# A state-space convolution by three products of 128-blocks in place of four, beside a quantized FFN

## The chip, the cores and the metric

The kernel runs on one core of one Trainium2 chip. The metric is the device time of one execution in microseconds (us), the median of several runs. The core has five engines with their own instruction queues: TensorE (PE, with its weight loads shown as PEld), VectorE (DVE), ScalarE (ACT), GpSimd (POOL) and SyncE (SP), which here only issues transfers. Engines wait for each other through semaphores.

## The reference, cut to what matters

The input `x` is 2048 rows (tokens) of 1024. The output is `x` plus two branches of its layer norm:

```
xn = layernorm(x)
x  = x + s4(xn) + ffn(xn)

# s4: K (1024 numbers) from the state matrices; D is one number
y = irfft(rfft(u, 2L) * rfft(K, 2L), 2L)[..., :L]      # causal convolution along the 1024 columns
s4 = y + D * u

# ffn: hidden 1024, inter 2752, int4 weights with a scale and zero per group of 64
h = silu(u @ Wg.T) * (u @ Wu.T)
ffn = h @ Wd.T
```

So each row is convolved with the same 1024 taps `K`: a product with an upper triangular Toeplitz matrix of 1024 x 1024. Cut into 128-blocks it has one block per diagonal, T0 to T7, and output block j is the sum over i <= j of x_i T(j-i).

## The kernel before, in words

The kernel is written in Python; a planner (the Tile framework) allocates buffers, adds semaphores and orders each engine's queue by the order of the program, a model of time, and hand-made order edges (`tc.issue_after`). Every number in a product is kept as a sum of two f16 numbers (high and low), and each product is three matmuls (`PASS`: high·high, high·low, low·high).

**Weights and FFN, to about 846 us.** The layer norm, the int4 unpacking and the gate and up products (`gate_up`) run here; `h` goes to HBM (`HF`, `HPL`), the down weights to `WD2`. In between, in small steps, `s4_kernel` computes `K` on 8 partitions; it ends with two tiny f32 matmuls into `s4k` and the stores of the split taps to HBM (`KP`, 128 zeros ahead of 1024 taps).

**The convolution, from 846.6 to 966.3 us.** This is the part that changes. It runs in two passes `cp` of 1024 rows. In a pass, `c` is a half of 512 rows, `q` one of its four tiles of 128 rows, and `hh` the half of the 1024 columns that is written, so there are 32 tiles of 128 x 512.

- `band` is loaded from `KP` with overlapping reads, four transfers on SP: its partition p is the tap vector shifted by p, so that any 128-block T_d is a slice of it.
- `diff` are two tables, differences of slices of `band`, built by DVE and ACT (`add_split`: three DVE instructions, an ACT cast and a DVE subtraction).
- `xs` are sums of blocks of `x` (blocks k and k + 2 of the first column half), two per `c`, built by the same `add_split`.
- `conv` opens a tile of 512 columns in a PSUM bank: the diagonal part as a staircase of four blocks (512, 384, 256 and 128 columns), and for hh = 1 the cross part with `diff`: four products of 256 columns. The cross part of 512 x 512 is thus done with three products of 256-blocks for four: two with difference tables, one shared.
- `last_tiles` adds five matmuls of 512 columns with `hpl` and `wp` (the last part of the FFN's down product), loads `x` into `o` (SP), and DVE evicts the bank onto it (`p<-cv`). For hh = 1 a second bank `pc` gets the shared product (`cc<-band,xs`, six matmuls of 256), which DVE adds to both halves of `o` (`p<-cc`). SP stores `o`.

In pass 0 `last_tiles` lags four tiles behind `conv` (list `behind`), in pass 1 none. The order of (c, hh) is (0,0), (0,1), (1,1), (1,0) in pass 0 and (0,1), (0,0), (1,1), (1,0) in pass 1. Each pass first loads `hpl` (768 KB, ACT's queue) and `x7` (1 MB, SP's queue), the transposed input of c = 1, hh = 0; the other three transposed inputs are in SBUF.

**The products, from 966.3 us.** 49 products of the FFN's down projection by a recursive scheme (`items`). `operands` loads `a` and, for the third product (m = 6), makes `s` and two differences on DVE; `gsplit` makes `g` (an ACT cast, a DVE subtraction). `prepare`, called once after each four tiles of pass 1, does this ahead for the first four.

**What is scarce.** PSUM has 8 banks, all in pool `psb`. Pool `f` has 6 buffers of 10 KB per partition, for `x7`, `xs`, `a` and `s`. Pool `hb` (tag `h`) has 10 of 2 KB, for `diff`, the temporaries `t` and `o`. Pool `g` has 5, `be` 3 (`band` and `wp`).

Lines: the profile shows nearly all instructions of the convolution under L77 and L82, the two lines of the helper `Engine` that issue them, so they are told apart by names: `cv`, `cc`, `xs`, `t`, `p`. POOL's instructions carry their own lines.

Of the kernel before, what the change touches and what calls it, by code (L numbers as in the profile page):

```python
# [24 lines left out]
F16 = mybir.dt.float16  # L25
# [4 lines left out]
ALU = mybir.AluOpType  # L30
# [57 lines left out]
def build(nc, tc, x, xp, raw_d, sz_d, par_d, vct_d, tab_d, csrow_d, out):  # L88
# [3 lines left out]
    with es:  # L92
# [13 lines left out]
        KP = dr.tile([2, 1280], F16, name="KP")  # L106

# [3 lines left out]
        def bank(name, tag="ps"):  # L111
            return psp.tile([P, 512], F32, tag=tag, name=name, **({} if tag == "ps" else {"bufs": 2}))
# [175 lines left out]
        with ea:  # L288
# [518 lines left out]
            def s4_kernel():  # L807
# [45 lines left out]
                tab, z, tab2 = tab[:, 0:512], tab[:, 512:896], tab2[:, 0:272]  # L853
                SP.dma_start(tab, tab_d[0])
                SP.dma_start(tab2[0:8], tab_d[1, 0:8, 0:272])
# [6 lines left out]
                yield "read"  # L862
                tc_, ts_ = tab2[0:8, 0:128], tab2[0:8, 128:256]
# [9 lines left out]
                pk = bank("s4k")[0:8, 0:128]  # L873
                with tc.issue_after(ends[0].ins):
                    PE.matmul(pk, tab2[0:8, 256:264], z[0:8, 0:128], start=True, stop=False)
                PE.matmul(pk, tab2[0:8, 264:272], z[0:8, 128:256], start=False, stop=True)
                yield "read"
                k = z[:, 256:384]
                V.tensor_copy(k[0:8], pk)
                V.scalar_tensor_tensor(k[0:1, 0:1], sm[0:1, 24:25], KS, k[0:1, 0:1], M, AD)  # L880
                kh = cst.tile([8, 2, P], F16, tag="s4kh", name="s4kh")
                split(kh, k[0:8])
# [4 lines left out]
                SP.dma_start(KP[:, 128:1152].rearrange("a (b c) -> b a c", b=8), kh)  # L887
# [296 lines left out]

        band = bep.tile([P, 2, 1024], F16, tag="be", name="band")
        for b in range(2):
            for n in range(2):
                p0 = 64 * b + 32 * n
                base = KP[:, 128 - 64 * b - 62 - n :]
                src = bass.AP(base.tensor, base.offset, [[2, 32], [base.ap[0][0], 2], [1, 1024]])  # L1190
                SP.dma_start(band[p0 : p0 + 32], src)

        def add_split(dst, srcs, op):

            (h0, l0), (h1, l1) = srcs
            n = dst.shape[2]
            t = htile("t")[:, 0:n]
            V.tensor_tensor(t, h0, h1, op)
            V.tensor_tensor(t, t, l0, ALU.add)
            V.tensor_tensor(t, t, l1, op)  # L1200
            A.copy(dst[:, 0], t)
            V.tensor_tensor(dst[:, 1], t, dst[:, 0], ALU.subtract)


        diff = []
        for a0, b0 in ((128, 384), (640, 384)):
            a, b = ([band[:, i, c : c + 384] for i in range(2)] for c in (a0, b0))
            diff.append(htile(f"diff{a0}").bitcast(F16).rearrange("p (a b) -> p a b", a=2)[:, :, 0:384])
            add_split(diff[-1], (a, b), ALU.subtract)
# [4 lines left out]

        def conv(cp, c, hh, q, xc):

            ts = slice(q * P, (q + 1) * P)
            ps = bank(f"cv{cp}{c}{hh}{q}")
            first = [True]

            def mm(dst, w, m):
                PE.matmul(dst, w, m, start=first[0], stop=False, skip_group_check=True)
                first[0] = False

            xt = xc[2 * c + hh]
            for k in range(4):
                for xi, bi in PASS:
                    mm(ps[:, P * k : 512], xt[:, xi, k, ts], band[:, bi, 0 : 512 - P * k])
            if hh:

                xt = xc[2 * c]
                for k in range(2):
                    for xi, bi in PASS:
                        mm(ps[:, 0:256], xt[:, xi, k + 2, ts], diff[0][:, bi, P - P * k : P - P * k + 256])
                for k in range(2):
                    for xi, bi in PASS:
                        mm(ps[:, 256:512], xt[:, xi, k, ts], diff[1][:, bi, P - P * k : P - P * k + 256])
            return ps

        def last_tiles(ps, cp, c, hh, q, hpl, xs):  # L1240

            ts = slice(q * P, (q + 1) * P)
            cols = slice(512 * hh, 512 * hh + 512)
            mm = lambda w, m, stop=False: PE.matmul(ps, w, m, start=False, stop=stop, skip_group_check=True)
            for hi, wi in PASS:
                mm(hpl[:, c, hi, ts], wp[0][:, wi, cols])
            mm(hpl[:, c, 2, ts], wp[1][:, 0, cols])
            mm(hpl[:, c, 2, ts], wp[1][:, 1, cols], True)
            t0 = 1024 * cp + 512 * c + P * q
            o = htile(f"p{cp}{c}{hh}{q}")  # L1250
            SP.dma_start(o, x[t0 : t0 + P, cols])
            V.scalar_tensor_tensor(o, ps, osc, o, ALU.mult, ALU.add)
            if hh:
                pc = bank(f"cc{cp}{c}{q}")
                for k in range(2):
                    for n, (xi, bi) in enumerate(PASS):
                        PE.matmul(pc[:, 0:256], xs[:, c, xi, k, ts], band[:, bi, 512 - P * k : 768 - P * k],
                                  start=(k == 0 and n == 0), stop=(k == 1 and n == 2))
                ov = o.rearrange("p (a b) -> p a b", a=2)
                V.scalar_tensor_tensor(  # L1260
                    ov, pc[:, 0:256].unsqueeze(1).to_broadcast([P, 2, 256]), osc, ov, ALU.mult, ALU.add)
            SP.dma_start(out[t0 : t0 + P, cols], o)
# [11 lines left out]

        for cp in range(2):
            home, tag = (gp, "g") if cp else (cvp, "cv")
            hpl = home.tile([P, 2, 3, 512], F16, tag=tag, name=f"hpl{cp}")
            A.dma_start(hpl, HPL[cp])
            x7 = fp.tile([P, 2, 4, 512], F16, tag="f", name=f"x7_{cp}")
            SP.dma_start(x7, XSP[cp])  # L1280
            xc = [xf[cp, 3], xf[cp, 1], x7, xf[cp, 0]]
            xs = fp.tile([P, 2, 2, 2, 512], F16, tag="f", name=f"xs{cp}")
            for c in range(2):
                for k in range(2):
                    a, b = ([xc[2 * c][:, i, m, :] for i in range(2)] for m in (k, k + 2))
                    add_split(xs[:, c, :, k, :], (a, b), ALU.add)

            behind = []
            for c, hh in ((0, 0), (0, 1), (1, 1), (1, 0)) if cp == 0 else ((0, 1), (0, 0), (1, 1), (1, 0)):
                for q in range(4):  # L1290
                    behind.append((conv(cp, c, hh, q, xc), cp, c, hh, q))
                    if len(behind) > 4 - 4 * cp:
                        last_tiles(*behind.pop(0), hpl, xs)
                if cp:
                    prepare()
            while behind:
                last_tiles(*behind.pop(0), hpl, xs)
# [207 lines left out]
```

## Time and profile before

| | |
|---|---|
| median of the runs shown | 1292.74 us (1290.92 to 1292.90, 3 runs) |
| profiled execution, own time | 1293.54 us |
| its span, first to last instruction | 1291.5 us |
| granted TensorE clock | 0.994 over the span, 1.00 in the convolution |
| PE busy | 1258.9 us, 97% |
| DVE, ACT, POOL busy | 1007.7, 672.1, 177.4 us |
| convolution | 846.60 to 966.34 us, 832 matmuls |
| DVE `p<-cv` x32, `p<-cc` x16 | 0.69 us each |
| DVE `t<-x` f32 from f16, 128x512 | 0.69 us |
| DVE `xs<-t,xs` f16, 128x512 | 0.69 us |
| ACT cast `xs<-t` 128x512 | 0.62 us |
| POOL add of 128x16 (line 323) | 0.22 us (median), up to 1.12 |
| POOL select of 128x128 (line 125) | 0.28 us |
| load `p<-in_x`, 256 KB | 3.7 us from issue to landing |
| load `x<-XSP`, 1 MB | 6.8 and 9.4 us from issue to landing |

How to read the profile: a row names the engine, the line, the operation, `out<-in` by the program's names, the shapes and the count; times are in us from the span's start; a bracket gives how long the engine had been idle and which instruction or transfer ended that. PE rows overlap, since matmuls are pipelined and their ends are modelled: what a matmul costs is the distance from its start to the next one's.

### The profile page before, as it was taken

Reading aid. Unit: us, or ns where it says so; the run is one execution under the profiler, and the core shown is the slowest. Engines: PE = TensorE matmul, PEld = TensorE weight load, DVE = VectorE, ACT = ScalarE, POOL = GpSimd, SP = SyncE. Lnnn points to the kernel's source line nnn. Section 1 sums busy time; section 2 is a strip of 40 time slices with the busy share of each in tenths; the row PEclk is TensorE's granted clock in tenths of the full one; section 3 lists DMA queues with packets and bytes.
Section 4 is the critical chain, followed back from the end, with each engine's and each line's share of the span. In section 5 each row is a group of like instructions: output and inputs, shape, how many; then the busy total and the mean of one; then the engine's idle time right before and its main releaser. Section 6 shows DMA issues by size and latency. Waiting matters only on the chain. (4 is left out here: it accounts for less than half of the span.)

```text
span 1291.5 us, 20871 instructions
## 1 busy us (share of the span) xinstructions
PE 1258.9 (97%) x7880; PEld 753.2 (58%) x7880; DVE 1007.7 (78%) x1344; ACT 672.1 (52%) x1208; POOL 177.4 (14%) x267
## 2 busy tenths in 40 slices
PE   5999999999999999999998999999999999999998
PEld 5744344444444444444443444456668888888887
DVE  6789974888978788878788887663758898779792
ACT  4868476666657556656666675620105433443330
POOL 2230010200010000100010001000000131356440
PEclk8999999999999999999999999999999999999999
DMA  6692938789795959889998998775938778999981
GB/s 222 147 227 59 203 101 157 213 218 239 162 252 144 253 146 241 224 209 235 244 239 216 260 243 201 226 264 183 350 122 344 239 230 226 256 283 259 288 176 50
DMA packets 358401, 276.04 MB, mean 214 GB/s; under 512 B 211668, under 2 KB 304668, under 8 KB 354204
## 3 DMA queue, kind: packets, MB, share of 16 engines
q1 hardware_dynamic: 335676, 261.59, 74.1%
q0 software_dynamic: 21760, 10.49, 6.9%
q10 hardware_dynamic: 864, 2.62, 0.5%
q8 instruction: 62, 1.02, 0.3%
q14 instruction: 39, 0.32, 0.1%
HBM read 132.36 MB, written 94.84 MB: 176 GB/s over the span
## 5 line engine op out<-in xcount | busy, mean ns | idle before, releaser
L82 PEld LDWEIGHTS <-wf 128*128 128x128 f16 x2807 | 274.0, 98 | 341.0 <-issue 7.0
L77 PEld LDWEIGHTS <-g 128*128 128x128 f16 x2940 | 287.7, 98 | 33.5
L82 ACT ACTIVATE w<-w,sz 128x64 f32<-128x64 int32 x560 | 196.0, 428 | 68.4 <-DVE w L82 51.3
L77 ACT CAST g<-a 128x2560 f16<-128x2560 f32 x42 | 97.5, 2324 | 176.6 <-PE A L77 50.4
L82 PE MATMUL D<-x,wf 128*128 128x512 f16 x816 | 188.0, 380 | 0.9 <-ACT D L82 0.9
L77 PE MATMUL A<-b,g 128*128 128x256 f16 x1680 | 185.9, 273 | 0.0
L82 PE MATMUL A<-x,wf 128*128 128x512 f16 x791 | 177.7, 380 | 5.1 <-DMA wf<-nat 4.7
L82 PE MATMUL C<-x,wf 128*128 128x512 f16 x804 | 179.1, 379 | 0.0
L82 DVE TENSOR_TENSOR w<-w 128x256 f32<-128x256 f32 (+1 forms) x244 | 132.6, 544 | 39.5 <-ACT w L82 32.3
L77 PEld LDWEIGHTS <-wf 128*128 128x128 f16 x1152 | 100.1, 100 | 98.4 <-DMA wf<-nat 4.3
L77 DVE TENSOR_TENSOR g<-a,g 128x2560 f16<-128x2560 f32 x42 | 118.5, 2823 | 29.6 <-ACT g L77 29.6
L1357 POOL DMA_DIRECT2D out<-o x64 | 78.8, 2127 | 320.7 <-DVE o L77 309.8
L82 ACT CAST nd<-w 128x896 f16<-128x896 f32 x70 | 65.2, 932 | 82.8 <-DVE w L82 65.6
L322 POOL TENSOR_SCALAR sz<-sz 128x16 f32<-128x16 f32 x42 | 16.5, 392 | 632.8 <-DMA sz<-in_sz 586.5
L77 PE MATMUL D<-b,g 128*128 128x256 f16 x840 | 94.0, 273 | 0.0
L82 PE MATMUL B<-x,wf 128*128 128x512 f16 x396 | 90.9, 379 | 2.1 <-ACT B L82 2.1
L82 DVE TENSOR_TENSOR nd<-w,nd 128x896 f16<-128x896 f32 x70 | 76.1, 1086 | 9.2 <-ACT nd L82 9.2
L82 ACT CAST nat<-w 128x896 f16<-128x896 f32 x62 | 55.2, 936 | 34.1 <-ACT B L82 17.0
L77 PEld LDWEIGHTS <-x 128*128 128x128 f16 x576 | 53.4, 98 | 25.0 <-issue 1.1
L82 DVE TENSOR_TENSOR nat<-w,nat 128x896 f16<-128x896 f32 x62 | 64.8, 1085 | 1.5 <-ACT nat L82 1.5
L77 PE MATMUL cv<-band,x 128*128 128x512 f16 (+3 forms) x384 | 57.1, 299 | 1.0 <-DVE hb L82 1.0
L77 DVE SCALAR_TENSOR_TENSOR p<-cv,p 128x512 f32<-128x512 f32 x32 | 22.0, 689 | 43.3 <-PE cv L77 33.6
(169 smaller groups left out, 1408.6 us busy)
## 6 DMA issues: line engine op xcount, KB each, us to landing
a<-HF SPq DMA_DIRECT2D x28, 1280.0 KB, 8.0
WD<-nd SPq DMA_DIRECT2D x70, 448.0 KB, 4.1
b<-WD SPq DMA_DIRECT2D x49, 640.0 KB, 6.0
w<-SZT SPq DMA_DIRECT2D x80, 256.0 KB, 5.4
raw<-in_raw SPq DMA_DIRECT2D x65, 256.0 KB, 4.0
HF<-ha SPq DMA_DIRECT2D x54, 256.0 KB, 3.4
HF<-s SPq DMA_DIRECT2D x40, 256.0 KB, 2.8
HF<-hb SPq DMA_DIRECT2D x36, 256.0 KB, 3.6
```

Source lines behind the costliest of these rows:

```text
L77: return method(*args, **kw)
L82: self.last = method(*args, **kw)
L322: G.tensor_scalar(sz[:, 0], sz[:, 0], WS, None, ALU.mult)
L1357: G.dma_start(dst, o[:, q], accum_op=ALU.add)
```

## The change

The convolution is cut into 128-blocks throughout, and the scheme of three products for four is applied both to the 256-blocks and, inside them and inside the diagonal staircase, to the 128-blocks.

- `s4_kernel` now makes 24 rows: the taps, and two sets of eight rows of differences of tap blocks. The rows of the last small product are differenced on POOL (copies, subtractions on 8 partitions, a memset); the term `D` comes in by a third tiny matmul in place of a DVE instruction. The differences go to HBM as `KQ` (two stores more).
- The function `toeplitz` loads `band` and, in eight transfers more on SP (rows of 128 taps), two tiles `parts` with eight 128-wide difference tables: `near` (2), `far` (2 x 2), `middle` (2). DVE and ACT build no `diff`.
- `block_sums` makes five sums of blocks per (cp, c) in place of two, one or fewer per tile (`sums_steps`), each by four DVE instructions and one ACT cast: an f32 sum of the high parts, the cast, the rest, an f16 sum of the low parts, and their addition. They are ordered behind the sum before the last and behind the last eviction (`emptied`).
- `conv`: the diagonal staircase keeps blocks 256, 128, 256 and 128 wide; for hh = 1 the cross part is four products of pairs of blocks with `far`, each matmul 128 wide (`crossed`).
- `last_tiles`: every tile has a second bank `pc` with the shared products (three matmuls of 128 columns for hh = 0; nine of 128 and six of 256 for hh = 1) and adds six matmuls of 128 with `near` to the first bank. DVE still evicts the first bank onto `o`; ACT evicts `pc` to `u`, scaled; POOL adds `u` to `o`, one add of 256 columns for hh = 0 and two of 512 for hh = 1; then SP stores `o`.
- The order in pass 0 is (0,0), (1,0), (0,1), (1,1), in pass 1 (0,0), (0,1), (1,0), (1,1). Both `x7` are loaded ahead of pass 0. Pool `f` holds two `x7` and four `xs` (one per cp and c).

The core of the diff:

```diff
+                G.tensor_copy(rows[:, 0:2, 0:8], tab2[0:8, 256:272].rearrange("p (a b) -> p a b", a=2))
+                G.tensor_copy(rows[:, 2, 0:8], ident[0:8, 0:8])
+                less = lambda dst, src, a, b, n=2: G.tensor_tensor(dst, src[:, :, a : a + n], src[:, :, b : b + n], SB)
...
-                    PE.matmul(pk, tab2[0:8, 256:264], z[0:8, 0:128], start=True, stop=False)
-                PE.matmul(pk, tab2[0:8, 264:272], z[0:8, 128:256], start=False, stop=True)
+                    PE.matmul(pk, rows[:, 0], z[0:8, 0:128], start=True, stop=False)
+                PE.matmul(pk, rows[:, 1], z[0:8, 128:256], start=False, stop=False)
+                PE.matmul(pk, rows[:, 2], one, start=False, stop=True)
...
+                for i in range(2):
+                    SP.dma_start(KQ[i].rearrange("a (b c) -> b a c", b=8), kh[8 + 8 * i : 16 + 8 * i])
...
         band = bep.tile([P, 2, 1024], F16, tag="be", name="band")
+        toeplitz(band, KP, [[1280, 2], [1, 1024]])
+        parts = []
+        for i in range(2):
+            t = htile(f"parts{i}").bitcast(F16).rearrange("p (a b c) -> p a b c", a=2, b=4)
+            toeplitz(t.rearrange("p a b c -> p (a b) c"), KQ[i], [[2 * P, 8], [1, P]])
+            parts += [t[:, :, k] for k in range(4)]
+        near, far, middle = parts[0:2], (parts[2:4], parts[4:6]), parts[6:8]
...
+        def block_sums(dst5, c, xc, sets):
+            add = ALU.add
+            for i in sets:
+                up, a, b = ((0, 0, 1), (1, 0, 1), (0, 2, 3), (0, 0, 2), (0, 1, 3))[i]
+                xt, dst, t = xc[2 * c + up], dst5[:, i], htile("t")
+                t16 = t.bitcast(F16)[:, 0:512]
...
+                    V.tensor_tensor(t, xt[:, 0, a], xt[:, 0, b], add)
+                A.copy(dst[:, 0], t)
+                V.tensor_tensor(dst[:, 1], t, dst[:, 0], ALU.subtract)
+                V.tensor_tensor(t16, xt[:, 1, a], xt[:, 1, b], add)
+                summed.append(V.tensor_tensor(dst[:, 1], dst[:, 1], t16, add))
+        def crossed(ps, xt, k, col, pair, ts):
+            for xi, bi in PASS:
+                for n in range(2):
+                    c0 = col + P * n
+                    PE.matmul(ps[:, c0 : c0 + P], xt[:, xi, k + 1 - n, ts], pair[n][:, bi],
+                              start=False, stop=False, skip_group_check=True)
...
             for k in range(4):
-                for xi, bi in PASS:
-                    mm(ps[:, P * k : 512], xt[:, xi, k, ts], band[:, bi, 0 : 512 - P * k])
+                lo, hi = P * k, 256 * (k // 2) + 256
+                for n, (xi, bi) in enumerate(PASS):
+                    PE.matmul(ps[:, lo:hi], xt[:, xi, k, ts], band[:, bi, 0 : hi - lo],
+                              start=(k == 0 and n == 0), stop=False, skip_group_check=True)
             if hh:
...
+                crossed(ps, xc[2 * c], 2, 0, far[0], ts)
+                crossed(ps, xc[2 * c], 0, 256, far[1], ts)
...
+            shared = [(256, 0, band[:, :, 256:384])]
+            if hh:
+                shared = [(384, 1, band[:, :, 256:384]), (256, 2, middle[0]), (384, 0, middle[1])]
+                for k in range(2):
+                    for n, (xi, bi) in enumerate(PASS):
+                        PE.matmul(pc[:, 0:256], xs[:, 3 + k, xi, ts], band[:, bi, 512 - P * k : 768 - P * k],
...
+            crossed(ps, xc[2 * c + hh], 0, 256, near, ts)
...
-            V.scalar_tensor_tensor(o, ps, osc, o, ALU.mult, ALU.add)
+            emptied.append(V.scalar_tensor_tensor(o, ps, osc, o, ALU.mult, ALU.add))
+            A.activation(u[:, used], pc[:, used], AF.Copy, scale=osc)
...
             if hh:
...
-                V.scalar_tensor_tensor(
-                    ov, pc[:, 0:256].unsqueeze(1).to_broadcast([P, 2, 256]), osc, ov, ALU.mult, ALU.add)
+                G.tensor_tensor(o.rearrange("p (a b) -> p a b", a=2), o.rearrange("p (a b) -> p a b", a=2),
+                                u[:, 0:256].unsqueeze(1).to_broadcast([P, 2, 256]), ALU.add)
+                G.tensor_tensor(ov, ov, u[:, 256:512].rearrange("p (a d) -> p a d", a=2).unsqueeze(2).to_broadcast([P, 2, 2, P]), ALU.add)
+            else:
+                G.tensor_tensor(ov[:, 1], ov[:, 1], u[:, 256:384].unsqueeze(1).to_broadcast([P, 2, P]), ALU.add)
             SP.dma_start(out[t0 : t0 + P, cols], o)
```

## The prediction

> **What bounds the kernel now.** I first read the table of busy time by stage, with edges at the convolution's first matmul, at its first product with `hpl`, and at the first FFN product.
>
> ```profile
> 846.60:857.11 10.51, 9.23 (x68) 5.86 (x67) 8.18 (x15) 2.51 (x5) 0.00 (x0) 1.00 0.84 287
> 857.11:902.96 45.85, 45.85 (x329) 30.81 (x330) 22.05 (x35) 3.06 (x5) 0.00 (x0) 1.00 0.63 206
> ...
> 907.28:966.34 59.06, 59.06 (x417) 38.68 (x416) 35.58 (x41) 4.76 (x4) 0.00 (x0) 1.00 0.63 223
> 966.34:1291.50 325.16, 321.12 (x2941) 287.57 (x2939) 256.23 (x172) 117.76 (x63) 98.40 (x80) 1.00 0.84 236
> ```
>
> The columns are length, then PE, PEld, DVE, ACT and POOL busy, the granted clock, DMA share. The convolution lasts 119.7 us (846.60 to 966.34) and PE is busy in all of it but 1.28 us, all at the start, at full clock. DVE has half of it free and POOL does nothing. So a matmul less is time less, as long as nothing new makes PE wait. A matmul's own duration is modelled (219 ns for 128 columns), so its price is the distance between starts. The PE timelines of three places give it:
>
> ```profile
> 50.49 0.83 PE L77 MATMUL g<-x,wf 128*128 128x128 f16 x12
> 51.16 0.83 PE L77 MATMUL u<-x,wf 128*128 128x128 f16 x12
> ```
> ```profile
> 966.34 6.71 PE L77 MATMUL A<-b,g 128*128 128x256 f16 x60
> 972.89 6.71 PE L77 MATMUL E<-b,g 128*128 128x256 f16 x60
> ```
> ```profile
> 875.64 4.02 PE cv L77 x29
> 879.66 0.66 PE cc L77 x6
> ...
> 893.03 2.71 PE cv L77 x17
> ```
>
> Twelve starts in 0.67 us are 56 ns for 128 columns, each with its own weight load; 6.55 us over 60 are 109 ns for 256. The last lines, from the chain of waits, are whole tiles: 4.02 + 0.66 us for an upper-half tile (hh = 1), 2.71 us for a lower one (hh = 0). The five `hpl` products in each, 512 wide, come 216 ns apart.
>
> **Matmuls.** Per pair of an hh = 0 and an hh = 1 tile, before costs 4.02 + 0.66 + 2.71 = 7.39 us. After, counted in the diff: hh = 0 has 6 matmuls of 256 and 6 of 128 on the diagonal, 3 of 128 shared, 6 of 128 `near`; hh = 1 the same 12, 12 of 128 `far`, 9 of 128 and 6 of 256 into `pc`, 6 of 128 `near`; both keep five of 512. That is 48 x 56 + 18 x 109 + 10 x 216 ns = 6.81 us. The difference, 0.58 us, times 16 pairs is **-9.2 us**. Columns fall by an eighth in the convolution proper, though matmuls rise from 832 to 1216. In the Trainium skill, "TensorE: Matmul & The Clock Gate", section "Back-to-back issue gap", a stream of weight load and matmul pairs is sustained at about 81 ns for 128 columns. By that figure 768 matmuls would cost 19 us more and the change would lose 10 us. This trace kept 56 ns through 192 such pairs between 50.5 and 62.7 us, so the sum goes by the trace.
>
> **The start of the stage.** The PE timeline:
>
> ```profile
> 846.60 1.79 PE L77 MATMUL cv<-band,x 128*128 128x512 f16 x12
> 849.40 6.68 PE L77 MATMUL cv<-band,x 128*128 128x512 f16 x48 [1.01 <-DVE hb L82]
> 855.92 0.93 PE L77 MATMUL cv<-diff,x 128*128 128x256 f16 x7
> 857.11 1.25 PE L77 MATMUL cv<-wp,hpl 128*128 128x512 f16 x5 [0.27 <-DMA hpl<-HPL]
> ```
>
> Five `conv` tiles hid the load of `hpl`, issued at 851.20 and landed 5.87 us later. After, the first five are all hh = 0, each 6 x 109 + 6 x 56 = 0.99 us, and the first tile's additions 9 x 56 = 0.50: 5.45 us of cover in the 10.51 us until 857.11. Idle would be 5.06 us, 3.8 more than now. If the order that the planner writes lets two more tiles into the two free banks, it is 1.8 more. `x7` of pass 0 is now needed at about 852.4, not after 858. In SP's queue eight table loads stand ahead of it (420 ns to issue, by `band`'s rows, 3.4 us together); it was issued at 838.81 and the two `x<-XSP` landed after 6.8 and 9.4 us, so it comes at 849.0 to 851.6, just in time. Pass 1's `x7`, 1 MB, moves from 857.93 to before all this and shares the DMA engines with `hpl`: up to 3 us later. The bounds are -1.3 (the present waits gone) and +7; I take **+3.0**, between the two cases with an unmoved `hpl`. The four subtractions and the casts per `diff` table leave DVE and ACT here; no PE wait hung on them, so this is worth nothing.
>
> **Block sums, DVE and POOL.** Twenty sums replace eight and the tables: by rows of this shape 0.69 + 0.69 + 2 x 0.42 = 2.23 us of DVE each (0.42 by the 128x256 f32 rows, as the f16 128x1024 takes 0.69 like f32 of 512), 44.5 us. The 16 `p<-cc` (0.69) leave DVE, the 32 `p<-cv` (22 us) stay. With some 8.5 us of the first products' 2.82 us instructions DVE has 75 us in 109. Evacuating `pc` is ACT's: about 0.6 us for 512 columns, with casts some 30 us of 109. Two free banks hide a late evacuation by one tile (2.6 us) in pass 0, three tiles in pass 1. POOL's 512-column add is not in the trace. The nearest row, POOL's 128x128 select at 0.28 us, times four gives 1.13 us, which I take; its slope over the 128x16 rows gives 0.49, and reading the second operand in turn 2.26. That is 16 x 2 x 1.13 + 16 x 0.56 = 45 us. What speaks against it:
>
> ```profile
> 286.56 2.11 DVE L82 TENSOR_TENSOR nat<-w,nat 128x896 f16<-128x896 f32 x2
> 286.84 0.89 POOL L323 TENSOR_TENSOR sz<-sz 128x16 f32<-128x16 f32 x1
> ```
> ```profile
> 802.39 0.68 DVE L82 TENSOR_TENSOR ha<-B,ha 128x512 f32<-128x512 f32 x1
> 802.60 0.22 POOL L323 TENSOR_TENSOR sz<-sz 128x16 f32<-128x16 f32 x1
> ```
>
> The same tiny add takes 0.89 us beside a DVE instruction with two SBUF operands, and 0.22 us beside one that reads PSUM. So POOL's adds and DVE's sums take turns: 45 + 44.5 + 8.5 = 98 us of 109, while `p<-cv` runs beside POOL. The Trainium skill says this more sharply in "SBUF — State Buffer", section "SBUF: two separate sides": the shared port pair is an exclusive lock held for a whole instruction. The row shows POOL's side; that DVE is held by a long POOL add no row here shows. It is tight in the last four tiles of pass 0 and the first of pass 1: 20.6 us of PE (8 x 2.57) against 8 sums (17.8) and adds of 4 x 2.26 + 4 x 0.56 = 11.3 us, 8.5 us too much, with 7.7 us (three tiles) of banks in hand. I take **+1.0** for PE waits here; between 0 and, at 2.26 us an add, some 30. The store now waits for POOL on SP, and loads `p<-in_x` queue behind it; eight buffers now hold two or three tiles per step instead of one. DVE waited 6.3 us for these loads and PE nothing; this lies in the same term.
>
> **The handover.** All six `f` buffers are now taken until the end (two `x7`, four sums).
>
> ```profile
> 955.71 2.82 DVE L77 TENSOR_TENSOR s<-a,a 128x2560 f32<-128x2560 f32 x1
> ...
> 969.64 2.82 DVE L77 TENSOR_TENSOR g<-a,g 128x2560 f16<-128x2560 f32 x1
> ```
>
> `s` started when `xs` was last read (955.51), 10.6 us before the stage's end E, and `g` of the third product was done at E + 6.1, needed at E + 13.1 (two products of 6.55). After, `s` waits for `x7` or the last sums, read until E - 2.6: three instructions of 2.82, an ACT cast of 2.33, `g`'s 2.82 and an eviction bring it to about E + 11.8, and the last tile's two adds can hold DVE 2.3 us. I take **+0.7**, between 0 and 3.5.
>
> **Elsewhere.** Two stores of `KQ`, one f32 matmul more and 13 tiny POOL instructions fall near 540 to 570 us. POOL idles about 19 us between scale steps there, which hides 13 x 0.2 to 1.2 us; the matmul that needs them came 15 us after that point. Nothing; without the cover, up to 15 us of late scales.
>
> **Sum.** -9.2 + 3.0 + 1.0 + 0.7 = -4.5 us. The profiled execution took 1293.54 us (span 1291.50 and 2.04 around it), so 1289.0 there; against the median shown, 1292.74, **1288.2 us**.
>
> **Rivals.** First, the cover is gone: the start costs 5.0 (PE keeps program order and `hpl` is 1.2 us late), the handover 2.0 and the banks 1.0. For it: no slack is left in either place. Against it: the planner moved matmuls past waiting transposes at 35 to 58 us. It gives -1.2, 1291.5 us. Second, POOL and DVE together become the bound, and the kernel is slower. Their turns fill 109 us when an add takes (109 - 53) / 40 = 1.40 us; from there each tenth costs 4 us. At 1.7 us the stage grows by 12 us, the sum is -9.2 + 3.0 + 0.7 + 12 = +6.5, 1299.2 us. For it: the 0.89 us row. Against it: four times the select stays below the point. Third, the change doesn't save what it counts: if a 128-column matmul cost as much as its weight load's 98 ns, 768 x 42 ns would be +32 us, 1320 us. Against it stand the 56 ns rows.
>
> **Chances.** Forecast 0.52 (alone 1284 to 1290), no cover 0.25, POOL's turns 0.21, weight loads 0.02. 0.2% (2.6 us) is about what a measurement of this kernel can tell from no change; the forecast gives faster, the first rival same, the others slower: 0.52, 0.25, 0.23. The range runs from 1283.5 (the 9.2 us whole) to 1298, which takes in the first rival and about half of the second.
>
> **What will show it.** `near`, `far` and shared matmuls 56 ns apart; PE idle of about 4 us before the first `wp,hpl` matmul, a few tenths elsewhere up to the products, about 1 us before the third product; POOL adds near 1.1 us, longer beside sums. Wrong would be: adds above 1.4 us, PE waiting for DVE `p` or ACT `u` in the middle, or matmuls near 80 ns.

## The result and the profile after

| | before | after |
|---|---|---|
| median, measured in turn on one chip (6 runs each) | 1292.51 us (1289.35 to 1294.62) | 1297.51 us (1296.19 to 1299.05) |
| ratio after to before, 95% interval | | 1.0042 [1.0027, 1.0057] |
| span of the profiled execution | 1291.5 us | 1295.2 us |
| granted clock over the span | 0.994 | 0.992 |
| convolution, first `cv` matmul to first product | 846.60 to 966.34: 119.75 us | 843.62 to 969.21: 125.59 us |
| first product to the end | 325.12 us | 325.97 us |
| POOL, DVE busy in the convolution | 0, 70.1 us | 58.1, 86.6 us |

The changed kernel is 0.42% slower; the forecast was 0.35% faster. The convolution became 5.84 us longer and the products 0.85 us. The span grew by only 3.7 us because the stage began 3.0 us earlier. How much of that lead belongs to the change is open: in the traced executions of the kernels below, which are equal to the kernel after ahead of the stage, it began anywhere from 842.4 to 847.7, and before was traced once.

Here are three rows of the table of busy time by stage for the kernel after (length; PE, PEld, DVE, ACT, POOL busy; clock; DMA share; GB/s):

```profile
871.00:908.70 37.70, 37.70 (x415) 29.55 (x413) 31.25 (x41) 10.24 (x20) 22.31 (x16) 1.00 0.50 162
908.70:929.30 20.60, 12.60 (x95) 8.70 (x94) 19.89 (x21) 7.36 (x9) 7.65 (x6) 0.75 0.85 317
929.30:969.21 39.91, 39.91 (x455) 32.20 (x454) 17.01 (x25) 7.20 (x15) 23.98 (x21) 1.00 0.64 212
```

The row 908.70:929.30 holds most of the damage (another wait for a bank, of 1.4 us, stands at 869). PE is busy for 12.60 of 20.60 us, the clock falls to 0.75, and DVE is busy for 19.89. In the row ahead of it DVE had been busy 31.25 of 37.70 us while PE still ran without a gap; the chain of waits, shown below, says that the backlog was building there, behind the two free banks. After it DVE is half idle. The average DVE load of the stage (86.6 of 125.6 us) hides this.

The PE timeline of that stretch:

```profile
907.91 1.15 PE L77 MATMUL cv<-band,x 128*128 128x256 f16 x12
911.07 0.33 PE L77 MATMUL cc<-band,xs 128*128 128x128 f16 x3 [2.01 <-DVE p L77]
911.23 0.50 PE L77 MATMUL cv<-parts,x 128*128 128x128 f16 x6
911.57 2.06 PE L77 MATMUL cv<-wp,hpl 128*128 128x512 f16 x5
913.42 2.06 PE L77 MATMUL cv<-band,x 128*128 128x256 f16 x12
...
924.71 1.76 PE L77 MATMUL cc<-band,xs 128*128 128x256 f16 x9 [5.99 <-DVE p L77]
```

PE waits twice for a bank, each time for the eviction `p<-cv` on DVE. The same twelve matmuls of 256 and 128 columns take 1.15 us at 907.91 and 2.06 us at 913.42: behind each wait the clock is halved for some 4 us. What DVE did meanwhile, from its timeline:

```profile
910.94 2.08 DVE L77 TENSOR_TENSOR t<-x 128x512 f32<-128x512 f16 x2
913.06 1.37 DVE L77 TENSOR_TENSOR xs<-xs,t 128x512 f16<-128x512 f16 x1
914.35 0.68 DVE L77 SCALAR_TENSOR_TENSOR p<-cv,p 128x512 f32<-128x512 f32 x1
914.95 0.68 DVE L77 TENSOR_TENSOR xs<-t,xs 128x512 f16<-128x512 f32 x1
915.55 3.16 DVE L77 TENSOR_TENSOR t<-x 128x512 f32<-128x512 f16 x2
...
921.23 2.83 DVE L77 TENSOR_TENSOR g<-a,g 128x2560 f16<-128x2560 f32 x1 [0.54 <-ACT g L77]
923.97 0.68 DVE L77 SCALAR_TENSOR_TENSOR p<-cv,p 128x512 f32<-128x512 f32 x1
```

Between two evictions (914.35 and 923.97) stand seven instructions of block sums and a subtraction of the first product's operand. DVE pauses only 0.54 us ahead of `g`, so the sums fill nearly all of the time. But the chain of waits, which from 883 to 910 runs along DVE, takes another path from there to the eviction:

```profile
904.63 0.68 DVE p L77
905.31 1.08 DVE t L77
906.39 1.69 DVE xs L77
908.11 1.37 DVE t L77
...
911.33 7.51 DMA a<-HF
918.87 2.34 ACT g L77
921.23 1.94 DVE g L77
```

The load of `a` landed, ACT cast it, DVE made `g`, and only then came the eviction, though the last sum had ended at 920.69. SP had issued this load at 911.33, behind a load of `x` whose buffer a block sum held until 910.42, and behind a store. So late sums delay the eviction in two ways: they stand ahead of it, and they make `a` late, whose `g` stands ahead of it too.

Some of the sums are far too long: the pair at 915.55 takes 3.16 us, where two `t<-x` take 0.69 + 0.42 us alone. The groups of the stage (busy us, mean ns) show who stretches whom:

```profile
L1295 POOL TENSOR_TENSOR p<-p,u 128x512 f32<-128x512 f32 x15 | 23.5, 1572 | 0.9
L77 DVE TENSOR_TENSOR xs<-t,xs 128x512 f16<-128x512 f32 x20 | 17.0, 854 | 6.3 <-ACT xs L77 6.2
L77 DVE TENSOR_TENSOR t<-x 128x512 f16<-128x512 f16 x20 | 16.2, 814 | 0.4
L77 DVE TENSOR_TENSOR t<-x 128x512 f32<-128x512 f16 x20 | 15.6, 786 | 0.0
L77 DVE TENSOR_TENSOR xs<-xs,t 128x512 f16<-128x512 f16 x20 | 10.4, 522 | 0.4
```

A block sum costs DVE 0.79 + 0.85 + 0.81 + 0.52 = 2.98 us on the average, not 2.23. One meeting, from the timelines of the two engines:

```profile
885.85 1.60 POOL L1295 TENSOR_TENSOR p<-p,u 128x512 f32<-128x512 f32 x1
886.35 1.38 DVE L77 TENSOR_TENSOR t<-x 128x512 f16<-128x512 f16 x1
```

DVE's f16 sum starts 0.5 us into POOL's addition and ends 0.28 us after it: 1.38 us, where it takes 0.42 alone. The addition takes 1.60, and 1.27 where it meets nothing. Both engines are held. An eviction, which reads PSUM and one tile of SBUF, keeps its 0.69 us throughout.

The start and the handover, from PE's timeline:

```profile
843.62 1.15 PE L77 MATMUL cv<-band,x 128*128 128x256 f16 x12
846.39 4.12 PE L77 MATMUL cv<-band,x 128*128 128x256 f16 x48 [1.62 <-DVE hb L82]
851.06 0.29 PE L77 MATMUL cc<-band,xs 128*128 128x128 f16 x2 [0.55 <-ACT xs L77]
...
984.19 2.03 PE L77 MATMUL A<-b,g 128*128 128x256 f16 x17 [0.84 <-DVE g L77]
```

**Where the time went.** Priced at the distances of the prediction (56, 109, 163 and 216 ns by width), the stage's matmuls are 118.18 us before and 108.96 after. From the distances between starts, PE's gaps are 1.60 us before and 12.95 after; 2.66 of these lie at the start, 10.29 in the middle. The half-clock time adds 3.7 (1.7 behind the first long wait, 2.0 behind the second). So -9.22 + 1.06 + 10.29 + 3.7 = +5.8 us for the stage.

### The profile page after: what moved, and what is told of

Read it like the earlier page. It is cut to its first block, busy times and chain, and to the rows that moved or that the text cites. A ratio compares the mean times of both kernels' runs of the same rounds, so it can differ in the third digit from the quotient of the medians.

```text
span 1295.2 us, 21856 instructions
## 1 busy us (share of the span) xinstructions
PE 1254.1 (97%) x8266; PEld 764.7 (59%) x8266; DVE 1032.3 (80%) x1367; ACT 691.0 (53%) x1250; POOL 248.5 (19%) x328
## 3 DMA queue, kind: packets, MB, share of 16 engines
q8 instruction: 65, 1.06, 0.3%
## 5 line engine op out<-in xcount | busy, mean ns | idle before, releaser
L77 PE MATMUL g<-x,wf 128*128 128x128 f16 (+1 forms) x336 | 48.8, 294 | 1.4 <-ACT wf L82 0.8
L77 PE MATMUL u<-x,wf 128*128 128x128 f16 (+1 forms) x336 | 47.4, 290 | 0.4 <-ACT wf L82 0.4
```

Of the source, the lines that this page charges most:

```text
L77: return method(*args, **kw)
```

## The experiments

Four theories were tried against each other. T1, turns: POOL's additions and DVE's instructions with two SBUF operands hold each other up, DVE falls behind from about 884 on, and evictions come late. T2, buffers: the store now waits for POOL, so the loads `p<-in_x` behind it come late (26.2 us of DVE idle time in the waits of the stage). T3, order: the first product's `g` stands ahead of evictions in DVE's order. T4, work: twenty sums are too much for DVE whatever POOL does. Stage length, gaps and half-clock time are taken from the one traced execution of each run as above, DVE's and POOL's busy time from the table by stage; every ratio is to the kernel before, run in turn with it on the same chip.

| kernel | median us | ratio [95%] | stage us | PE gaps | half clock | DVE, POOL busy in it |
|---|---|---|---|---|---|---|
| after | 1297.51 | 1.0042 [1.0027, 1.0057] | 125.6 | 12.95 | 3.7 | 86.6, 58.1 |
| no_adds | 1284.0 | 0.9939 [0.9915, 0.9963] | 114.9 | 6.06 | 0 | 70.6, 0 |
| h13 | 1295.69 | 1.0024 [1.0014, 1.0034] | 125.0 | 13.2 | 2.8 | 86.4, 58.8 |
| late_prepare | 1297.69 | 1.0038 [1.0023, 1.0053] | 126.2 | 15.3 | 1.9 | 86.4, 57.2 |
| sums_on_act | 1302.0 | 1.0073 [1.0055, 1.0090] | 129.7 | 17.0 | 3.7 | 31.1, 52.2 |
| side_adds | 1293.36 | 1.0012 [1.0000, 1.0024] | 122.5 | 11.6 | 1.9 | 84.6, 47.5 |
| dve_adds | 1293.67 | 1.0012 [0.9999, 1.0025] | 122.3 | 11.6 | 1.7 | 94.7, 0 |
| mixed_adds | 1297.58 | 1.0039 [1.0024, 1.0054] | 127.5 | 16.7 | 1.9 | 91.6, 21.7 |
| g_behind | 1299.93 | 1.0057 [1.0035, 1.0080] | 121.9 | 11.6 | 1.4 | 87.6, 58.4 |
| spread | 1295.11 | 1.0013 [1.0000, 1.0026] | 122.2 | 10.6 | 2.7 | 83.5, 60.0 |
| spread_dve | 1287.2 | 0.9946 [0.9929, 0.9962] | 114.9 | 6.09 | 0 | 94.3, 0 |
| spread_dve2 | 1287.02 | 0.9950 [0.9932, 0.9969] | 115.8 | 6.95 | 0 | 94.9, 0 |
| upper_only | 1285.02 | 0.9930 [0.9912, 0.9949] | 112.2 | 1.14 | 0 | 89.8, 0 |

### no_adds: POOL's additions left out

```diff
-            ov = o.rearrange("p (a b d) -> p a b d", a=2, b=2)
-            if hh:
-                G.tensor_tensor(o.rearrange("p (a b) -> p a b", a=2), o.rearrange("p (a b) -> p a b", a=2),
...
-                G.tensor_tensor(ov[:, 1], ov[:, 1], u[:, 256:384].unsqueeze(1).to_broadcast([P, 2, P]), ALU.add)
```

> The changed kernel without POOL's additions of u to o; ACT still evicts pc into u, SP stores o. Left out: the shared products are missing in the output. Theory 1 (POOL's adds and DVE's two-operand instructions take turns: a block sum takes 2.98 us of DVE in the changed kernel against 2.23 by its shapes, DVE is busy 51 of 58 us from 871 to 929 us, and evictions come late): sums return to 2.2 us, PE's idle time from 908 to 929 us (8.0 us, and 4 to 5 us at half clock after it) nearly goes, time about 1285 us. Theory 2 (too few buffers of pool hb: loads of x late, DVE waits 26 us for them): buffers also come free 3 us earlier, part of the gain, about 1291 us. Theory 3 (the first product's operand, loaded late, holds ACT and DVE in order): unchanged, about 1296 us.

Against after, 13.5 us of the medians go. In the traced execution, the slowest of the four, the stage is 10.7 us shorter. The four kinds of sum instruction return to their length alone:

```profile
L77 DVE TENSOR_TENSOR t<-x 128x512 f32<-128x512 f16 x20 | 13.6, 683 | 0.0
...
L77 DVE TENSOR_TENSOR t<-x 128x512 f16<-128x512 f16 x20 | 8.4, 422 | 0.3
```

All the rest of the change is in this kernel, the twenty sums, the ACT evacuations and the new order, and it is faster than before. So POOL's additions are what turned the result, and T4 alone is out. But the kernel takes away two things at once, POOL's hold on DVE and the additions' place between eviction and store.

### h13: thirteen buffers in `hb`, not ten

```diff
-        pools["h"] = poolb("hb", bufs=10)
+        pools["h"] = poolb("hb", bufs=13)
```

> The changed kernel with 13 buffers in pool hb in place of 10, the most that fit. Theory 2 (buffers): DVE's waits for loads of x fall from 26 us to below 10, the stalls at 869 and 909 us (1.3 and 2.2 us) go, about 1292 us. Theory 1 (turns): nothing changes in what DVE has to do, about 1296 us. Theory 3: about 1296 us.

The 6.2 us wait shrank to 5.5, the stage by 0.6 us, the median by 1.8. DVE's idle time for loads of `x` ahead of evictions fell only from 26.2 us to 12.4, so this run takes away only half of what T2 names. no_adds says more: there DVE idles 23.1 us for these loads, and the kernel is faster than before. So that idle time by itself costs little.

### late_prepare: the first products' operands prepared one block later

```diff
                 if cp:
-                    prepare()
+                if cp and (c, hh) != (0, 0):
+                    prepare()
...
             while behind:
...
+            if cp:
+                prepare()
```

> The changed kernel with the four calls that prepare the first products' operands moved one block of four tiles later in pass 1 (the last one behind the block's end). Theory 3 (the cast and the subtraction of the first product's g stand in ACT's and DVE's queues before evictions while their load, issued at 911 us, is under way): the 6.2 us wait at 918 us and the half clock behind it go, the handover may lose 1 to 3 us, about 1290 us. Theory 1: the DVE backlog stays and the wait shrinks by at most the 2.8 us of the subtraction, about 1294 us.

The order that the planner wrote has `g` in the same place, so this run says nothing on T3; the wait at 918 was 8.1 us.

### sums_on_act: two ACT copies for each block sum

```diff
-                    V.tensor_tensor(t, xt[:, 0, a], xt[:, 0, b], add)
-                A.copy(dst[:, 0], t)
-                V.tensor_tensor(dst[:, 1], t, dst[:, 0], ALU.subtract)
-                V.tensor_tensor(t16, xt[:, 1, a], xt[:, 1, b], add)
-                summed.append(V.tensor_tensor(dst[:, 1], dst[:, 1], t16, add))
+                A.copy(dst[:, 0], xt[:, 0, a])
+                A.copy(dst[:, 1], xt[:, 1, a])
```

> The changed kernel with the 20 block sums replaced by two ACT copies each of one of the two blocks (high and low part), so DVE makes no sums. Left out: the sums, so the shared products have wrong stationary operands. Theories 1 and 4 (DVE's load, made of the sums and of their turns with POOL's adds): DVE falls from 97 us to about 45 us in the stage, all waits in the middle go, about 1286 us, and POOL's adds fall to 1.27 us of 512 columns. Theory 2 (buffers): loads of x stay late, waits of 2 to 4 us remain, about 1291 us.

The time is useless as a test of T4, because the planner put the copies ahead of the FFN's last work on ACT, and PE stood still at the start, as its timeline shows:

```profile
857.78 2.50 PE L77 MATMUL cv<-band,x 128*128 128x256 f16 x14 [12.31 <-DVE hb L82]
```

The other side of the meeting can be read from it, though. With no sums on DVE, POOL's additions of 256 columns take 725 ns on the average in this run; in after they take 928:

```profile
L1294 POOL TENSOR_TENSOR p<-p,u 128x256 f32<-128x256 f32 x16 | 11.5, 725 | 94.9 <-issue 73.7 <-DVE p L77 21.3
```

### side_adds: POOL adds beside the path

```diff
-                G.tensor_tensor(o.rearrange("p (a b) -> p a b", a=2), o.rearrange("p (a b) -> p a b", a=2),
...
+                for a in range(2):
+                    G.tensor_tensor(u, u, u, ALU.add)
             else:
-                G.tensor_tensor(ov[:, 1], ov[:, 1], u[:, 256:384].unsqueeze(1).to_broadcast([P, 2, P]), ALU.add)
+                G.tensor_tensor(u[:, 256:512], u[:, 256:512], u[:, 256:512], ALU.add)
```

> The changed kernel with POOL's additions put beside the chain: POOL adds u to itself (the same number of adds of the same width), o is stored right after DVE's eviction. ACT copies 128 columns more per hh = 0 tile so that all of u is written. Left out: the shared products are missing in the output. If the adds cost by taking turns with DVE's block sums (theory 1): sums stretch again to about 3 us each and the stalls at 908 and 918 us stay, 1294 us or more. If they cost by standing between the eviction and the store (late stores, late buffers, SP's queue): near the kernel without adds, about 1285 us.

POOL does as many additions of the same width, but onto `u`, and no store waits for them. With one tile for all operands they are shorter, 1.04 us alone where those of after take 1.27, so POOL is busy for 47.5 us and not 58.1. Against after, 3.1 us of the stage go; against no_adds, 7.5 us stay. The sums are still stretched, by 0.71 us each (2.93 for 2.22), though nothing of the path goes through POOL:

```profile
L77 DVE TENSOR_TENSOR t<-x 128x512 f16<-128x512 f16 x20 | 14.7, 741 | 0.3
...
L77 DVE TENSOR_TENSOR xs<-xs,t 128x512 f16<-128x512 f16 x20 | 12.9, 643 | 0.4
```

So of the stage's 10.7 us that POOL's additions cost, turns alone, with additions a fifth shorter, cost 7.5; the 3 us left are their place between eviction and store together with the longer additions. The 6.1 us that PE waits at 914 end behind `g`, though, not behind a sum (DVE's timeline):

```profile
916.74 2.82 DVE L77 TENSOR_TENSOR g<-a,g 128x2560 f16<-128x2560 f32 x1 [3.02 <-ACT g L77]
```

DVE had its sums done at 913.72 and idled for the cast. In no_adds it idles 4.5 us at the same place, but PE waits only 1.6: there the load of `a` was issued 59.4 us after the stage's start, here 64.9. What the turns cost reaches PE in part this way.

### dve_adds: DVE adds `pc` from PSUM, POOL does nothing

```diff
-            A.activation(u[:, used], pc[:, used], AF.Copy, scale=osc)
+            onto = lambda dst, src, n: V.scalar_tensor_tensor(
+                dst, src.unsqueeze(1).to_broadcast([P, 2, n]), osc, dst, ALU.mult, ALU.add)
             if hh:
...
+                onto(o.rearrange("p (a b) -> p a b", a=2), pc[:, 0:256], 256)
+                for a in range(2):
+                    onto(ov[:, a], pc[:, 256 + P * a : 384 + P * a], P)
             else:
...
+                onto(ov[:, 1], pc[:, 256:384], P)
```

> The changed kernel with pc added onto o by DVE straight from PSUM (one instruction of 512 and two of 256 columns for hh = 1, one of 256 for hh = 0), with no u, no ACT eviction of pc and nothing on POOL. Theory 1: sums go back to 2.2 us, but DVE gets 16 x (0.69 + 3 x 0.42) = 31 us more on 76, so 107 us of work in a stage of 109: DVE becomes the bound in the hh = 1 blocks, about 1290 to 1294 us. If only POOL's place in the chain mattered: about 1285 us.

No instruction is stretched any more, and the kernel is level with before. But a 7.4 us gap stands at 913, without any POOL. This run's table by stage, and DVE's timeline:

```profile
908.70:929.30 20.60, 13.39 (x135) 10.66 (x133) 18.70 (x30) 7.03 (x6) 0.00 (x0) 0.83 0.83 308
```
```profile
913.60 0.42 DVE L77 TENSOR_TENSOR xs<-xs,t 128x512 f16<-128x512 f16 x1
913.95 5.60 DVE L77 TENSOR_TENSOR g<-a,g 128x2560 f16<-128x2560 f32 x2
920.28 0.69 DVE L77 SCALAR_TENSOR_TENSOR p<-cv,p 128x512 f32<-128x512 f32 x1 [0.74 <-DMA b<-WD]
```

The additions' work now lies on DVE itself (94.7 us busy), and the same stretch is too full: 5.6 us of it are the two `g`, ahead of the eviction as T3 says. T1 is not the whole: what PE waits for is a DVE that has more to do between two evictions than the free banks cover, and a turn is one way to fill it.

### mixed_adds: half of the additions on each

```diff
+                A.activation(u[:, 256:512], pc[:, 256:512], AF.Copy, scale=osc)
+                onto(o.rearrange("p (a b) -> p a b", a=2), pc[:, 0:256], 256)
                 G.tensor_tensor(ov, ov, u[:, 256:512].rearrange("p (a d) -> p a d", a=2).unsqueeze(2).to_broadcast([P, 2, 2, P]), ALU.add)
             else:
+                onto(ov[:, 1], pc[:, 256:384], P)
```

> The changed kernel with the adds shared out: DVE adds pc straight from PSUM for hh = 0 (256 columns) and the first half of it for hh = 1 (512 columns); POOL keeps the second add of hh = 1, ACT evicts only that half. POOL falls from 60 to about 24 us, DVE gets 16 x (0.42 + 0.69) = 18 us more. Theory 1: turns fall by more than half and DVE stays below 100 us, about 1288 us. If every POOL add in the store chain costs alike: about 1291 us.

It is as slow as after: PE has a gap of 11.2 us at 912.6, in which DVE makes both `g` one after the other and idles 1.9 and 0.4 us for their casts ahead of the eviction (its timeline):

```profile
917.32 2.83 DVE L77 TENSOR_TENSOR g<-a,g 128x2560 f16<-128x2560 f32 x1 [1.87 <-ACT g L77]
920.53 2.83 DVE L77 TENSOR_TENSOR g<-a,g 128x2560 f16<-128x2560 f32 x1 [0.39 <-ACT g L77]
923.27 0.68 DVE L77 SCALAR_TENSOR_TENSOR p<-cv,p 128x512 f32<-128x512 f32 x1
```

POOL is busy for 21.7 us here and for 58.1 in after, and nothing is gained: the loss doesn't go by the number of turns alone. What PE waits for is `g`.

### g_behind: the operands of the products ordered behind the evictions

```diff
-            A.activation(u[:, used], pc[:, used], AF.Copy, scale=osc)
+            evicted.append(A.activation(u[:, used], pc[:, used], AF.Copy, scale=osc))
...
-                    prepare()
+                    with tc.issue_after(emptied[-1].ins), tc.issue_after(evicted[-1].ins):
+                        prepare()
```

> The changed kernel with each of the four preparations of a product's operand in pass 1 ordered on DVE and ACT behind the last eviction of the four tiles before it. Theory 3 (the operand's cast and subtraction ahead of evictions): the wait of 6.2 us at 918 us and the half clock after it go, about 1289 us. Theory 1: the backlog of sums ahead of the eviction stays, the wait shrinks by the 2.8 us of the subtraction and what ACT waits for the load, about 1294 us.

The one wait of 6.2 us becomes two, of 2.7 us at 920 and 2.0 at 949, and the stage is 3.7 us shorter. The products take 329.1 us instead of 326.0, since `g` is late there, and the clock is halved for 3.4 us at 984. What the eviction at 920 now waits for is neither a sum (the last ended at 919.9) nor `g`, but the load of `x` (DVE's timeline):

```profile
922.50 0.69 DVE L77 SCALAR_TENSOR_TENSOR p<-cv,p 128x512 f32<-128x512 f32 x1 [2.61 <-DMA p<-in_x]
```

T3 names what stood in the way at that moment, but moving it only moves the wait.

### spread: the sums of pass 1 in pass 1

```diff
             while behind:
-                next(summing, 0)
                 finish()
```

> The four block sums that stand between the last four tiles of pass 0 go into the first eight tiles of pass 1; number of instructions and POOL's additions unchanged. If the stalls at 908.8 (2.2 us) and 918.5 (6.2 us) come from the crowding of sums among the evictions of that stretch, they shrink to 1 us each at most and the half-clock time behind them (about 4 us of matmul time lost) goes too: stage 125.6 to about 118, time about 1290. If it is the whole of DVE's work with POOL's turns in this stage that is too much, wherever the sums stand, the wait only moves into pass 1's later tiles or to the first product: stage 123 or more, time 1296 to 1299.

The last evictions of pass 0 now follow each other in DVE's order, and the four sums go between the tiles of pass 1. The waits for evictions around 908 to 925 are gone, but PE now waits for the sums themselves, as its timeline shows:

```profile
916.29 0.38 PE L77 MATMUL cc<-band,xs 128*128 128x256 f16 x2
918.89 0.50 PE L77 MATMUL cc<-band,xs 128*128 128x256 f16 x3 [2.22 <-DVE xs L77]
922.01 0.71 PE L77 MATMUL cc<-band,xs 128*128 128x256 f16 x4 [2.62 <-DVE xs L77]
```

The stage lies between the two expectations, the median nearer to that of the rival: with POOL's turns, an order without crowding is worth 2.4 us by the medians and 3.4 by the stage.

### spread_dve: the same order, and no POOL

> The same place of the sums, and the additions made by DVE from PSUM as in dve_adds, POOL idle. DVE has 105 us of work in dve_adds against 109 us of matmuls. If turns and crowding together are the whole loss, stage about 115 to 117 and time 1287 to 1289; if DVE's sum of work alone is the bound, the 7.4 us wait of dve_adds stays or moves and the time is 1293 to 1295.

Both edits together (those of spread and of dve_adds). Here is this run's table by stage:

```profile
871.20:935.00 63.80, 63.80 (x722) 51.05 (x720) 57.66 (x109) 11.98 (x14) 0.00 (x0) 1.00 0.73 254
935.00:942.00 7.00, 4.23 (x38) 2.75 (x36) 4.58 (x10) 0.62 (x1) 0.00 (x0) 1.00 0.83 270
```

PE is without a gap for 63.8 us, though DVE is busy for 57.7 of them. Neither edit alone brought the time under that of before; together they bring 0.96% against after (1.0042 to 0.9946), where each alone brought 0.3% (1.0013 and 1.0012). Of that, 0.96 - 0.59 = 0.37% comes only when both are made; four ratios with intervals of 0.13 to 0.17% each way leave this some 0.3% uncertain, so that it is likely and not more.

### spread_dve2: more buffers and a later `hpl` load

```diff
-        pools["h"] = poolb("hb", bufs=10)
+        pools["h"] = poolb("hb", bufs=13)
...
-                A.copy(dst[:, 0], t)
+                copied.append(A.copy(dst[:, 0], t))
...
-            A.dma_start(hpl, HPL[cp])
+            with tc.issue_after(copied[3].ins) if cp else nullcontext():
+                A.dma_start(hpl, HPL[cp])
```

> As spread_dve, with 13 buffers of the output size for 10 and pass 1's hpl load issued behind the fourth cast of the sums on ACT, not ahead of them all. If late loads and the ACT queue at the start of the stage are what is left, 1.5 to 3 us better than spread_dve (1285 to 1287); if DVE's backlog is what is left, within 1 us of it.

Within 0.2 us of spread_dve. The gaps at 935 to 941, all waits for DVE's evictions, shrank from 3.25 to 2.5 us. At the start the wait for the cast behind the `hpl` load (0.9 us) is gone, but PE then waited for pass 0's `hpl` itself, which came 6.4 us after its issue at 848.55 (PE's timeline):

```profile
854.94 1.25 PE L77 MATMUL cv<-wp,hpl 128*128 128x512 f16 x5 [2.50 <-DMA hpl<-HPL]
```

So the run doesn't decide between its two expectations: of the 6.95 us of gaps that are left, 2.7 are a load and 2.5 are DVE's evictions.

### upper_only: the lower tiles as in the kernel before

```diff
-                lo, hi = P * k, 256 * (k // 2) + 256
+                lo, hi = P * k, 256 * (k // 2) + 256 if hh else 512
...
-            pc = bank(f"cc{cp}{c}{hh}{q}")
-            shared = [(256, 0, band[:, :, 256:384])]
+            pc = bank(f"cc{cp}{c}{hh}{q}") if hh else None
+            shared = []
...
-            crossed(ps, xc[2 * c + hh], 0, 256, near, ts)
+            if hh:
+                crossed(ps, xc[2 * c + hh], 0, 256, near, ts)
...
-            else:
-                onto(ov[:, 1], pc[:, 256:384], P)
```

> As spread_dve2, but the lower tiles (hh = 0) are computed as in the kernel before, with four products and no cc bank, no addition: 16 additions of 256 columns fewer on DVE (about 6 us), 3 x 128 columns more of matmul in each of 16 tiles (16 x 3 x 56 ns = 2.7 us). If DVE is the bound of the stage, 2 to 4 us better than spread_dve2; if TensorE is, 2 to 3 us worse.

Three products for four in the upper tiles only: 2.2 us of matmuls more (111.17 against 108.96), DVE busy for 5.1 us less (89.8 against 94.9), and the stage is 3.6 us shorter than in spread_dve2. PE waits 1.14 us at the start and then never (this run's table by stage):

```profile
844.80:871.20 26.40, 25.42 (x203) 16.45 (x202) 19.53 (x37) 5.72 (x10) 0.00 (x0) 1.00 0.84 274
871.20:957.01 85.81, 85.81 (x873) 64.21 (x871) 70.29 (x126) 12.68 (x15) 0.00 (x0) 1.00 0.69 242
```

This is faster than both kernels: 1285.02 us, 0.9930 [0.9912, 0.9949] of before. Against spread_dve2 the medians differ by 2.0 us, the intervals of the ratios overlap, and the gain has two causes. Of the 5.8 us of gaps that are gone, 2.5 were waits for DVE's evictions in the middle, about what the 2.2 us of matmuls cost. The other 3.3 lie at the start: the longer lower tiles cover the load of `hpl` (2.7) and the wait for a bank behind the first tile, which is longer too, is 0.65 us shorter. So the last matmuls saved bring about what their vector work costs, and that the kernel is faster still is owed to cover at the start, as far as one trace of each shows.

## Why the prediction was wrong

- **Matmuls, -9.2:** right. 118.18 us became 108.96, and the distances of before hold: over the 37.70 us from 871.00 on PE has no gap and the trace stays on that count. The 81 ns for each 128-column pair that the Trainium skill states ("TensorE: Matmul & The Clock Gate", section "Back-to-back issue gap") didn't show; the third rival is out.
- **The start, +3.0:** it cost 1.06 us. The wait that was foreseen ahead of the first `hpl` matmul (3.8 us more) didn't come: the planner wrote one more tile of `conv` (twelve matmuls) ahead of it, and `hpl` landed 4.6 us after its issue and not 5.9. This second half is luck: PE came to `hpl` just as it landed (a wait of 0.2 us), and in spread_dve2, where it took 6.4 us, the wait did come, with 2.5 us. Pass 0's `x7` was issued ahead of the table loads and not behind them. Instead PE waited 0.6 us longer for a bank at 844.8 and 0.7 us for a cast of the sums on ACT, which stood behind pass 1's `hpl` load in ACT's queue.
- **Block sums, DVE and POOL, +1.0:** this is the step that failed. It measured 10.29 us of gaps and 3.7 us at half clock, 14.0 in all. Three things in it were off. First, POOL's addition of 512 columns takes 1.27 us alone and 1.5 on the average here, held by DVE; the select's row, times four, gave 1.13. Second, the text left open whether a long POOL addition holds DVE, and priced DVE's sums at 2.23 us; held by POOL they took 2.98, 15 us more for twenty. Third, the place was named rightly, the last four tiles of pass 0 and the first of pass 1, and 8.5 us too much was worked out for it, but 7.7 us (three tiles) of banks in hand were set against that, though the text itself gave pass 0 one tile. These banks were not in hand: DVE had been behind since 884 (31.25 of 37.70 us busy in 871.00 to 908.70; the chain of waits runs along its sums, their casts and its evictions from 883.35 to 910.42, with one pause for a store), the evictions come in DVE's program order behind the sums, and the first two products' `g` (2.83 us each) stand in the same stretch and were left out of the local sum. So were the eight evictions (8 x 0.69 = 5.5 us): they run beside POOL, but they take DVE's time, and with them and both `g` DVE alone has 17.8 + 5.5 + 5.7 = 29.0 us to do in 20.6. no_adds, side_adds and spread_dve bear this out, each by its part.
- **The half clock** behind the long waits was in no step: 3.7 us of slower matmuls. Only the 2.0 us behind the second wait surely lengthen the stage, since PE has no gap after them; the 1.7 behind the first ended ahead of the 6.2 us wait, and without them PE would have come to that wait earlier.
- **The handover, +0.7:** right, 0.85 us by the length of the products, and PE's one wait for a `g` behind the second product is 0.84 us. The preparation met POOL as was foreseen: an addition that starts within a DVE instruction of 2560 columns (970.49 to 973.78) takes 3.85 us, and the next such instruction, which starts within that addition, takes 3.77 us instead of 2.82 (timelines of POOL and DVE):

```profile
971.05 3.85 POOL L1293 TENSOR_TENSOR p<-p,u 128x512 f32<-128x512 f32 x1
```
```profile
973.81 3.77 DVE L77 TENSOR_TENSOR a<-s,a 128x2560 f32<-128x2560 f32 x1
```

- **The rivals.** The second one happened, POOL's and DVE's turns. Its point, 1.40 us an addition, was worked out from the whole stage (109 us), for an addition that nothing holds. By that account 1.27 us still leaves room: 16 x (2 x 1.27 + 0.72) + 44.5 + 8.5 = 105 us. It was decided by the 20 us in which the work is crowded, and there the point lies lower: dve_adds shows the same gap with no POOL in it.

Two rules of the Trainium skill can be read beside this. "SBUF — State Buffer", section "SBUF: two separate sides", has the port pair as an exclusive lock held for a whole instruction by whichever engine starts first. The meetings at 885.85 and 971.05 agree with it, for both engines, and so do the evictions, which take one operand from PSUM and kept their 0.69 us. "TensorE: Matmul & The Clock Gate", section "HAM oscillation — how this bites in real kernels", puts the limit at idle gaps of about 3.4 us. Here a wait of 2.01 us was followed by half clock (911.57), and one of 2.50 us in spread_dve2 by none; no one length of gap fits these runs.

What stays open: how much of the 6.2 us wait is the sums themselves and how much `g` and its late load, since each was only moved and never taken away by itself, and the late load is partly the sums' doing; how the 10.7 us divide between the turns and the additions' place, since side_adds has shorter additions; and why the clock fell after some waits and not after others of the same length.

## What to carry to other kernels

Before work is put on an idle engine, ask what the busy one loses by it: here 52 us of additions on an idle POOL cost DVE 15 us of longer sums and the stage 10.7, by their turns and by their place ahead of the store. Sum an engine's work over the stretch in which it is crowded and in its program order, not over the stage, and count banks in hand only if the engine that frees them isn't already behind. And when a scheme saves matmuls at the price of vector work, try it on the part where one saved matmul costs least of that work: with the additions on DVE in both, the upper tiles alone were 0.70% under before, the whole scheme 0.50%, a difference within the noise, and by the traces owed mostly to the start of the stage.

## What the runs showed of the hardware

- A POOL addition of 512 f32 columns with both operands in SBUF takes 1.27 us alone, mostly 1.60 beside block sums, 3.7 to 3.9 beside DVE's 2560-column instructions; one of 256 takes 0.72.
- DVE is held as well: 0.42 us became 1.38, 0.69 up to 1.75. The evictions, which read PSUM, are not: 0.69 us in each.
- TensorE's clock was halved for 3.3 to 4.4 us of matmuls behind waits of 2.0 and 6.0 us (after), 2.5 (g_behind) and 8.1 (late_prepare): twelve matmuls took 2.06 us instead of 1.15. In after the matmuls behind the two waits took 1.7 and 2.0 us longer.
- 128-column matmuls, each with its own weight load, kept 56 ns: in before in streams from 50.5 to 62.7 us, and in the stage after, 768 of them among wider ones, wherever PE had no gap and the full clock.
